# A prologue reordered: inputs by feature chunk, layer norm first, shared expert ahead of the router

## The chip, the cores and the metric

The kernel runs on one core of one Trainium2 chip. The metric is the device time of one execution in microseconds (us), median of several runs. Before the change it is 1330.2 us (three runs, 1329.89 to 1331.93).

## What is computed

A sequence x (8 batches, 512 steps, 256 features, float32) passes through four blocks; each adds its output to x. A second input, cond (8 by 256), steers three of them.

```python
# L0: mixture of experts, one shared (hidden 512), 8 routed (hidden 128), top 2
shared = (silu(x @ sw1.T) * (x @ sw3.T)) @ sw2.T
s = sigmoid(x @ router_w.T + cond @ router_t_w.T)
combine = gates of the two largest s + router_bias, normalised
routed = sum_e combine[e] * (gelu(x @ rw1[e].T) @ rw2[e].T)
x = x + (shared + routed) / 3
# L1: wavelet transform, gate = sigmoid(silu(cond@W1.T+b1)@W2.T+b2), inverse
# L2: low-rank matrices made per batch from cond (layer norm, gelu, then W2 of 8 MB)
# L3: a GRU over the 512 steps
Z = sigmoid(xz + H @ Whz.T); R = sigmoid(xr + H @ Whr.T)
H = Z * H + (1 - Z) * tanh(xh + R * H @ Whh.T);  Y = H @ Whq.T
```

The wavelet step with its inverse comes down to scaling by a gate per feature, so the kernel holds it as the factor `lr2`.

## The kernel before, in words

Features lie on partitions (two chunks k of 128, `KC`), batches and time steps in the free dimension. Time is cut into 16 windows of 32 steps (`WS`, `NW`); a window is 256 columns (8 batches times 32 steps). L0 to L2 of a window are a list of jobs (`window_jobs`); L3 is a loop over 512 steps that needs the window's result.

There are two phases. The **prologue** loads the weights, computes what depends on cond alone (time bias of the router, layer norm and the low-rank matrices of L2, the gate of L1), routes the first four windows (`route`, `EARLY = 4`) and computes window 0. The **recurrence** then runs the GRU step by step and fills the gaps of every step with jobs of later windows.

The order of instructions on each engine is fixed when the program is built. A `Job` has an engine, the jobs that it depends on, the ring buffers that it uses, and an estimated duration (`takes`, and `lag` for transfers). `Jobs.run` (line 179) keeps a clock for each engine and, whenever the clock of an engine has come, emits the first job of its queue that is ready by these estimates. The estimates only choose the order; on the chip each engine works through its own list in order, and semaphores make it wait for what an instruction really needs. So an instruction that waits holds up everything behind it on its engine. A second set of queues, `small`, is not looked at by `run` before the change.

Names and lines that matter here:

- `load_x` (347) loads a stretch of x, one transfer for each chunk k. Block 0 is `x0`, four windows; its first window is loaded first (364), the rest at 367. `sw13_sb` (365) holds sw1 and sw3, loaded as two transfers, one per matrix. Then follow rw1 (371), sw2 (373), wsq_a (375, five square matrices), rw2 (377), and the eight 1 MB pieces of W2 (`pieces`, 380 to 387, tile w, five buffers: a sixth piece waits until an earlier one has been used). I call them w1 to w8. All these go through SP's queue. Small inputs (cond, router, router bias, vecs, bias2 as b) go through ACT's queue, h0 and the bias rows through POOL's.
- `hidden` (525): the two products x·w of a hidden block, into one half of a PSUM pair (tiles hp and low); line 453 is the helper `quads` that issues each product as four matrices of 32 columns. A shared unit (540) is hidden w1, hidden w3, sigmoid on ACT (546), lin and g on DVE (554, 562), then `into_acc` (505) into the accumulator acc. A routed unit (570) is hidden, Erf on ACT (578), gl on DVE (586), g on POOL (594: gl times bc), then `into_acc`.
- `route` (789): logits (799), transpose on DVE (825), sigmoid (829), some twenty small DVE operations for the top 2 (836 to 862), a transpose to cT (825); cT is written to DRAM (comb_d, 877) and read back broadcast to all partitions (bc, 485). For the first four windows (`via_pool`) POOL and ACT issue these.
- layer norm (887 to 940): mean by TensorE (892), diff (903), dsq (907), var (911), square root on ACT (917), `normalize`. `dense_cond` (942) makes hid and the gate, with products at 953 and hid_pre, g_pre, gate_pre at 963.
- the low-rank matrices (1000 to 1061): bias rows (misc<-b, by `quads`), then four uses of the pieces in pairs, (w1, w2) to (w7, w8), at 1023 (misc<-w), low_out (1039), transposes (1048), low_in (1054).
- `jobs.run` at 1074 ends the prologue when window 0's L0, low_in, and the last weights have been placed. The steps after that (window 0's L2, xt, the first projection at 1115) are emitted by the second `run`, at 1231.

Of the kernel before, what the change touches and what calls it, by code (L numbers as in the profile page):

```python
# [9 lines left out]
F32 = mybir.dt.float32  # L10
# [6 lines left out]
P = 128  # L17
B, T, C = 8, 512, 256
KC = C // P
E = 8  # L20
# [116 lines left out]
class Jobs:  # L137
# [41 lines left out]
    def run(self, until):  # L179

        while any(j.done is None for j in until):
            for eng, at in self.clock.items():
                if at <= self.now:
                    job = next((j for j in self.queues[eng] if j.ready(self.now)), None)
                    if job is not None:
                        self.queues[eng].remove(job)
                        job.emit(self.now)
                        self.clock[eng] = self.now + job.takes
# [11 lines left out]
def cond_resid_kernel(  # L200
# [109 lines left out]
    jobs = Jobs()  # L310

# [35 lines left out]
    def load_x(n, mb, some=None):  # L347
# [8 lines left out]
        a, b = (i * WS for i in some)  # L356
        for k in range(KC):
            got = load(t[:, k, :, a:b], xs[:, k, :, t0 + a : t0 + b], mb)
# [5 lines left out]
    load_x(0, 0.25, (0, 1))  # L364
    sw13_sb = const.tile([P, 2, KC, HS], F32, name="sw13_sb")
    got_sw13 = [load(sw13_sb[:, g], rows_of(sw13[g]), 0.5) for g in range(2)]
    load_x(0, 0.4, (1, EARLY))
    got_vec = load(vec, vecs, 0, eng="ACT")
    got_b2 = load(b2[: 4 * R], bias2.rearrange("q (r d) -> (q r) d", d=C), 0, eng="ACT")
    rw1_sb = const.tile([P, KC, E, P], F32, name="rw1_sb")  # L370
    got_rw1 = load(rw1_sb.rearrange("p k e h -> p k (e h)"), rows_of(rw1), 1.0)
    sw2_sb = const.tile([P, HC, C], F32, name="sw2_sb")
    got_sw2 = load(sw2_sb, rows_of(sw2), 0.5)
    wsq_a = const.tile([P, KC, 5, C], F32, name="wsq_a")
# [90 lines left out]
    def window_jobs(w, routed, xt, via_pool=False):  # L465
# [18 lines left out]
        def fetch(i):  # L484
# [12 lines left out]
                lag=LAG,  # L497
# [27 lines left out]
        def hidden(lazy, n, lhs, got):  # L525
            last = None
            for k in range(KC):
                last = mm(
                    lazy,
                    n,  # L530
                    lambda k=k: lhs(k),
                    lambda k=k: x[:, k],
                    k == 0,
                    [last, got, got_x[w]],
                )
            return last
# [3 lines left out]
        for m in range(HC):  # L540
            h, sig, lin, g = bank(), Lazy(r_sig), Lazy(r_lin), Lazy(r_g)
            j1 = hidden(h, 0, lambda k, m=m: sw13_sb[:, 0, k, ts(m, P)], got_sw13[0])
            j3 = hidden(h, 1, lambda k, m=m: sw13_sb[:, 1, k, ts(m, P)], got_sw13[1])
# [26 lines left out]
        for e2 in range(0, E, 2):  # L570
            h = bank()
            for n in range(2):
                e = e2 + n
                j = hidden(h, n, lambda k, e=e: rw1_sb[:, k, e, :], got_rw1)
# [15 lines left out]
                    [h, sig, gl],  # L590
                )
# [153 lines left out]

    prod = set1.tile([P, KC, B, E], F32, name="prod")
# [42 lines left out]
    def route(ws, tiles, psum, via_pool, behind=()):  # L789
# [6 lines left out]
        def products():  # L796
# [12 lines left out]
            products, [*(got_x[w] for w in ws), got_rout_sq, *behind], [logits], 0.45  # L809
# [655 lines left out]
```

## Time and profile before

| | us |
|---|---|
| median of the runs | 1330.2 |
| the profiled execution, its own time | 1334.46 |
| its span, first to last instruction | 1332.2 |
| first product of x (tile hp) | 8.26 |
| transpose of the logits | 16.78 |
| cT done, POOL writes comb_d | 25.32 |
| first routed g on POOL | 36.88 |
| the four uses of pieces of W2 start (PE misc, L1023) | 31.23, 38.12, 42.51, 48.06 |
| window 0's accumulator complete | 53.50 |
| recurrence starts (grh<-wx) | 67.8 |
| mean granted clock of TensorE | 0.984 |

The execution that was profiled took 1334.46 us, 2.3 us more than its span: that much lies around the first and the last instruction. It also lies 4.3 us above the median of the runs.

How to read it: PE is TensorE's matmul row, PEld its weight loads, DVE, ACT and POOL the vector, scalar and GpSimd engines, SP the queue that issues most transfers. A float32 product counts as two instructions per matrix, so a product in `quads` is x8 in the trace. A tile is named without its buffer's number: grh is also the name that small prologue results have (they borrow a bank of it). The chain of waits is followed back from the last instruction; asked for a stretch, it starts from that stretch's end.

### The profile page before, as it was taken

The page shows a single profiled execution, that of the slowest core. Times are in us where ns is not written, and L with a number is a line of the kernel's source. Part 1 is how long each engine was busy: PE and PEld are TensorE (multiplying, and loading weights), DVE is VectorE, ACT ScalarE, POOL GpSimd, SP SyncE. Part 2 cuts the span into 40 slices and gives each one's busy share as a digit, 9 for nine tenths or more (in the row PEclk, how much of TensorE's full clock was granted, in tenths as well). Part 3 has the DMA queues.
Part 4 walks back from the last instruction along what each step waited for, and adds up shares of the span by engine and source line. Part 5 has one row for each costly group of instructions (what it writes and reads, how often), then busy time and mean ns, then how long its engine had stood idle before and what let it go on. Part 6 is the DMA issues. An engine that isn't in the chain of part 4 may idle for free.

```text
span 1332.2 us, 88576 instructions
## 1 busy us (share of the span) xinstructions
PE 1183.3 (89%) x39016; PEld 704.9 (53%) x39016; DVE 914.9 (69%) x6255; ACT 507.3 (38%) x3403; POOL 149.3 (11%) x228
## 2 busy tenths in 40 slices
PE   8999989999898998989898988888888888988885
PEld 4565555555555555555454554545454554555554
DVE  5267777777776767666676767667676766767665
ACT  2143433343343434334343434434343443433332
POOL 3310111101010110101011010101101010110000
PEclk8999999999999999999999999999999999989997
DMA  9910001101010000201000010100001000000111
GB/s 338 330 51 13 4 6 44 44 5 36 5 41 15 20 20 4 52 4 28 12 21 20 4 36 4 28 12 20 20 4 36 4 4 4 5 4 4 36 36 19
DMA packets 41586, 46.44 MB, mean 35 GB/s; under 512 B 27472, under 2 KB 31088, under 8 KB 40048
## 3 DMA queue, kind: packets, MB, share of 16 engines
q1 hardware_dynamic: 38304, 38.31, 9.6%
q8 instruction: 304, 4.98, 1.5%
q0 software_dynamic: 1184, 2.31, 0.6%
q14 instruction: 82, 0.67, 0.2%
q10 hardware_dynamic: 1712, 0.16, 0.1%
HBM read 36.45 MB, written 4.33 MB: 31 GB/s over the span
## 4 chain that ended last, share of the span: by engine, by line
PE 68%; DVE 17%; ACT 8%; issue 5%; DMA 1%; POOL 0%; DVEq 0%; ACTq 0%; POOLq 0%
PE grh L1115 34%; PE hp L453 13%; PE acc L453 8%; DVE rT L1295 6%; DVE d L1295 5%; PE gz L1115 5%; ACT r L1281 5%; PE low L453 4%; ACT c L1281 3%; PE misc L453 3%; DVE s_h L1372 2%; DVE s_rh L1312 2%; DMA brow<-in_bias_rows_dram 0%; DMA bc<-comb_d 0%; PE misc L1023 0%
## 5 line engine op out<-in xcount | busy, mean ns | idle before, releaser
L1281 ACT ACTIVATE r<-grh 128x32 f32<-128x32 f32 x1024 | 146.3, 195 | 439.8 <-PE grh L1115 439.8
L1295 DVE STREAM_TRANSPOSE rT<-r 128x32 f32<-128x32 f32 x1024 | 156.0, 190 | 225.6 <-ACT r L1281 221.6
L1115 PE MATMUL grh<-wh,s_h 128*32 128x64 f32 x8192 | 223.8, 226 | 75.4 <-DVE s_h L1372 74.2
L1115 PEld LDWEIGHTS grh<-wh,s_h 128*32 128x32 f32 x8192 | 145.0, 110 | 274.4 <-DVE s_h L1372 271.2
L1115 PE MATMUL grh<-wh,s_rh 128*32 128x64 f32 x8192 | 223.1, 227 | 52.0 <-DVE s_rh L1312 29.8
L1281 ACT ACTIVATE c<-grh 128x32 f32<-128x32 f32 x1024 | 146.3, 195 | 310.0 <-PE grh L1115 307.6
L1115 PEld LDWEIGHTS grh<-wh,s_rh 128*32 128x32 f32 x8192 | 141.6, 109 | 201.5 <-DVE s_rh L1312 198.9
L1295 DVE STREAM_TRANSPOSE d<-c 128x32 f32<-128x32 f32 x1024 | 156.5, 192 | 119.3 <-ACT c L1281 113.5
L1115 PE MATMUL gz<-wh,s_h 128*32 128x64 f32 x8192 | 212.1, 221 | 1.2 <-issue 1.2
L1115 PEld LDWEIGHTS gz<-wh,s_h 128*32 128x32 f32 x8192 | 155.3, 111 | 1.7 <-issue 1.6
L453 PE MATMUL hp<-x,sw_sb 128*32 128x256 f32 x2016 | 151.8, 389 | 1.7 <-ACT sig L546 1.1
L594 POOL TENSOR_TENSOR g<-gl,bc 128x256 f32<-128x256 f32 x128 | 93.6, 733 | 518.1 <-DVE s_h L1372 355.6
L453 PE MATMUL hp<-x,rw_sb 128*32 128x256 f32 x2016 | 149.6, 380 | 2.3 <-ACT sig L578 1.1
L453 PE MATMUL acc<-g,rw_sb 128*32 128x256 f32 x2048 | 150.2, 379 | 1.6 <-POOL g L594 1.1
L1372 DVE TENSOR_TENSOR_SCAN s_h<-d,d 128x16 f32<-128x16 f32 x1024 | 145.3, 183 | 0.0
L1312 DVE TENSOR_TENSOR s_rh<-rT,s_h 128x8 f32<-128x8 f32 x1024 | 133.1, 167 | 0.0
L1295 DVE STREAM_TRANSPOSE zT<-z 128x64 f32<-128x64 f32 x512 | 121.6, 238 | 1.1 <-ACT z L1281 1.1
L1281 ACT ACTIVATE z<-gz 128x64 f32<-128x64 f32 x512 | 121.0, 236 | 1.9 <-PE gz L1115 1.4
L1115 PE MATMUL grh<-wx,xt 128*32 128x128 f32 x2048 | 106.8, 276 | 3.3 <-ACT r L1281 3.3
L1386 ACT COPY hist<-s_h 128x16 f32<-128x16 f32 x512 | 105.9, 207 | 0.5 <-DVE s_h L1372 0.5
L1324 DVE TENSOR_TENSOR d<-zT,s_h 128x16 f32<-128x16 f32 x512 | 90.8, 177 | 17.6
L1325 DVE TENSOR_SCALAR d<-zT 128x16 f32<-128x16 f32 x512 | 86.8, 170 | 0.0
(151 smaller groups left out, 1193.4 us busy)
## 6 DMA issues: line engine op xcount, KB each, us to landing
bc<-comb_d SPq DMA_DIRECT2D x56, 256.0 KB, 3.2
w<-in_w_dram SPq DMA_DIRECT2D x8, 1024.0 KB, 12.6
out_dram<-x SPq DMA_DIRECT2D x14, 256.0 KB, 3.2
x<-in_xT_dram SPq DMA_DIRECT2D x2, 1536.0 KB
rw_sb<-in_rw_dram SPq DMA_DIRECT2D x2, 1024.0 KB
bc<-comb_d POOLq DMA_DIRECT2D x8, 256.0 KB, 8.4
sw_sb<-in_sw_dram SPq DMA_DIRECT2D x3, 512.0 KB, 6.3
wsq_a<-in_sq_a_dram SPq DMA_DIRECT2D x1, 1280.0 KB
```

The source lines that it names most:

```text
L453: nc.tensor.matmul(out[ts(j, 32)], lhs[:, ts(j, 32)], rhs, start=start, stop=False, skip_group_check=True,)
L594: lambda gl=gl, g=g, e=e: nc.gpsimd.tensor_tensor(g.get(), gl.get(), bcs[e // 2].get()[:, e % 2], ALU.mult),
L1115: nc.tensor.matmul(out[ts(j, 32)], lhs, rhs[:, ..., ts(j, FQ)], start=start, stop=False, skip_group_check=True,)
L1281: nc.scalar.activation(x, y, func)
L1295: ins = nc.vector.transpose(dst.rearrange("p i u b -> p i (u b)"), src.rearrange("p (i r) -> p i r", r=32),)
L1312: prod = tt(s_rh[u][:, k, u, :], rT[:, k, u, :], h[:, k], ALU.mult)
L1324: tt(d1[:, :, u, :, 1], zT[:, :, u, :], h, ALU.mult)
L1325: nc.vector.tensor_scalar(d0[:, :, :, 1], zT[:, :, u, :], -1.0, 1.0, ALU.mult, ALU.add)
L1372: new = nc.vector.tensor_tensor_scan(s_h[v][:, k, v].rearrange("p b w -> p (b w)"), d0[:, k].rearrange("p b w -> p (b w)"), d1[:, k, u].re ...
L1386: nc.scalar.copy(hist[:, :, t, :], s_h[v][:, :, v, :, 1])
```

## The change

It does these things:

1. sw1 and sw3 are loaded by feature chunk: x chunk 0, then chunk 0 of both matrices, x chunk 1, then chunk 1 (`load_sw13`, `between`). The tile's layout changes with it. Products wait only for their own chunk (`got[k]`, `got_x[w][k]`), and the second hidden of a shared or routed pair no longer starts its own accumulation group (`first`).
2. sw2 is loaded ahead of rw1, and rw1 in two halves of four experts each.
3. The layer norm's jobs, up to the square root, are put ahead of the router's. The rest of the normalisation stays where it was.
4. The router's top-2 operations, and gl of window 0, go into the `small` queue, and `run` now looks at `small` after the main queue. So lin, g, hid_pre and the like go ahead of them when ready.
5. Estimates that steer the order are changed: PE's clock starts at 3.5, the lag of the comb_d writes is 1.8 times, that of the bc fetches 2 times what it was, durations of loads are raised.
6. The bias rows of the low-rank matrices (misc<-b) depend on the load of wsq_a as well.

In the order of instructions that comes of it: on PE, misc<-b moves from ahead of the first product to behind the layer norm's dense product; the first products run k = 0 of two units, then k = 1 of both; the router's products come behind the first half of the third unit; routed units of window 0 are done before the accumulations of routed experts, and three of those stand between the third and the fourth use of pieces, five behind the fourth. On ACT, one of three table loads is gone (square root is first), and the comb_d writes move behind three more activations. On POOL, three of the four fetches for window 1 move ahead of the first routed g. On SP, the two sw13 transfers alternate with x. From window 1's first products on, the order is as before.

```diff
@@ Jobs.run
-                    job = next((j for j in self.queues[eng] if j.ready(self.now)), None)
+                    qs = (self.queues[eng], self.small[eng])
+                    ready = ((j, q) for q in qs for j in q if j.ready(self.now))
+                    job, q = next(ready, (None, None))
                     if job is not None:
-                        self.queues[eng].remove(job)
+                        q.remove(job)
@@
     jobs = Jobs()
+    jobs.clock["PE"] = 3.5
@@ load_x
+        got = []
         for k in range(KC):
-            got = load(t[:, k, :, a:b], xs[:, k, :, t0 + a : t0 + b], mb)
+            got.append(load(t[:, k, :, a:b], xs[:, k, :, t0 + a : t0 + b], mb))
+            if between is not None:
+                between(k)
@@
-    load_x(0, 0.25, (0, 1))
-    sw13_sb = const.tile([P, 2, KC, HS], F32, name="sw13_sb")
-    got_sw13 = [load(sw13_sb[:, g], rows_of(sw13[g]), 0.5) for g in range(2)]
-    load_x(0, 0.4, (1, EARLY))
+    sw13_sb = const.tile([P, KC, 2, HS], F32, name="sw13_sb")
+    got_sw13 = []
+
+    def load_sw13(k):
+        rows = sw13[:, ts(k, P), :].rearrange("g p h -> p g h")
+        got_sw13.append(load(sw13_sb[:, k], rows, 0.5))
+
+    load_x(0, 0.6, (0, 1), load_sw13)
+    load_x(0, 0.5, (1, EARLY))
@@
-    rw1_sb = const.tile([P, KC, E, P], F32, name="rw1_sb")
-    got_rw1 = load(rw1_sb.rearrange("p k e h -> p k (e h)"), rows_of(rw1), 1.0)
     sw2_sb = const.tile([P, HC, C], F32, name="sw2_sb")
     got_sw2 = load(sw2_sb, rows_of(sw2), 0.5)
+    rw1_sb = const.tile([P, KC, E, P], F32, name="rw1_sb")
+    half = slice(0, E // 2), slice(E // 2, E)
+    got_rw1 = [
+        load(rw1_sb[:, :, e], rw1.rearrange(...)[:, :, e], 0.5)
+        for e in half
+    ]
@@ fetch of bc
-                lag=LAG,
+                lag=2 * LAG if via_pool else LAG,
@@ hidden
-        def hidden(lazy, n, lhs, got):
-            last = None
+        def hidden(lazy, n, lhs, got, first=None):
+            made = []
             for k in range(KC):
-                last = mm(
+                made.append(mm(
...
-                    k == 0,
-                    [last, got, got_x[w]],
+                    k == 0 and first is None,
+                    [first, *made, got[k], got_x[w][k]],
@@ gl of a routed unit
+                    queue=None if w else jobs.small,
@@ route
-            queue = jobs.queues if via_pool else jobs.small
-            d = jobs.add("DVE", fn, [d, got_rbias], (), takes, queue)
+            d = jobs.add("DVE", fn, [d, got_rbias], (), takes, jobs.small)
...
-        made = []
+        made, lag = [], 1.8 * LAG if via_pool else LAG
@@ layer norm: mean_over_features ... sd0 stand ahead of prod and time_bias, not behind route
@@ biased_rows
-        j = pe(biased_rows, [got_b2], [gp], 0.45)
+        j = pe(biased_rows, [got_b2, got_sq_a], [gp], 0.45)
```

## The prediction

> **What bounds the kernel now.** I read the page first, for which engine carries the end.
>
> ```profile
> PE 1183.3 (89%) x39016; PEld 704.9 (53%) x39016; DVE 914.9 (69%) x6255; ACT 507.3 (38%) x3403; POOL 149.3 (11%) x228
> ...
> PE 68%; DVE 17%; ACT 8%; issue 5%; DMA 1%; POOL 0%; DVEq 0%; ACTq 0%; POOLq 0%
> ```
>
> TensorE is busy for 89% of the span and holds 68% of the chain that ended last. Most of that is the recurrence, from 67.8 us to the end. The order of instructions there is the same before and after: on PE all rows from the window-1 products that follow the last expert's accumulation, on DVE, ACT and POOL likewise. So the change can move the end only by moving the start of the recurrence, and I need the chain up to there. This is the chain of work in order of time (start, duration, what):
>
> ```profile
> 25.32 5.02 DMA comb_d<-cT
> 30.34 0.28 issue
> 30.63 6.12 DMA bc<-comb_d
> ...
> 36.88 0.73 POOL g L594
> ...
> 42.69 1.73 PE misc L1023 x32
> ...
> 48.24 1.73 PE misc L1023 x32
> 49.97 0.86 PE acc L453 x16
> 50.84 0.37 PE grh L1048 x2
> 51.21 2.29 PE acc L453 x40
> 53.50 2.59 PE hp L453 x48
> ...
> 67.79 0.22 PE grh L1115 x8
> ```
>
> The gates cT are written out at 25.32, come back as bc at 36.78, and from 37.66 PE works almost without a break until window 0's accumulator is complete at 53.50. From there to the recurrence at 67.79 are 14.3 us of unchanged steps. Call 53.50 the end of the prologue; that is the number to predict. Next, engines by stretch (PE, PEld, DVE, ACT, POOL busy; granted clock; DMA share; GB/s):
>
> ```profile
> 5.50:9.00 3.50, 2.06 (x24) 1.33 (x23) 0.64 (x4) 0.00 (x0) 2.25 (x5) 0.99 1.06 338
> 9.00:15.80 6.80, 6.29 (x56) 3.05 (x60) 2.36 (x11) 3.16 (x4) 3.20 (x6) 0.50 1.12 347
> ...
> 24.00:31.00 7.00, 6.50 (x92) 4.12 (x91) 4.56 (x21) 1.48 (x5) 0.90 (x2) 1.00 1.01 419
> 31.00:37.00 6.00, 4.97 (x83) 2.61 (x82) 0.54 (x3) 1.33 (x4) 1.96 (x5) 1.00 1.01 418
> 37.00:53.50 16.50, 15.68 (x272) 8.84 (x276) 4.85 (x22) 1.87 (x6) 7.70 (x12) 1.00 0.99 329
> ```
>
> Two things are to be seen. PE has slack at the front: half clock from 9.0 to 15.8, and 1 us idle in 31 to 37. The last column but one is the second limit: the DMA engines are full from 5.5 us on, at 419 GB/s in 24 to 31. The waits of SP's queue name what it carries:
>
> ```profile
> SPq L317 <- PE misc L1023: 12.9, 2, 6.8
> SPq L317 <- DMA wsq_a<-in_sq_a_dram: 9.0, 1, 9.0
> ```
>
> The eight 1 MB pieces w1 to w8 of the low-rank matrix are loaded in five buffers; the sixth and the eighth wait until PE has used earlier ones. By the completion records in the trace w1 to w4 land at 26.36, 28.80, 31.24 and 33.67 (2.44 apart), then, with the bc fetches beside them, w5 36.90, w6 40.93, w7 43.49, w8 47.19. PE's fourth use of pieces (48.24) needs w8, so DMA is only 1 us behind PE there.
>
> **First products (gain).** Before, PE's first product hp stands behind misc<-b, which waits for b (landed 7.69): it starts at 8.26. After, misc<-b is moved behind the dense products and the first products need only half of x and half of sw13. Those land about 6.5 (the first half of sw13 landed at 7.75, behind one more 128 KB of x that took 1.1 us), so PE starts behind the time bias, at 6.7. The second half of sw13 still lands last, 9.48. Products that need it run from 9.5.
>
> **Clock.** The row 9.00:15.80 shows PE busy 6.29 us at clock 0.50: some 3.1 us of work lost. The Trainium skill ("TensorE: Matmul & The Clock Gate", Part 1: The HAM clock gate) says that the clock is halved after an idle window of about 3.4 us. Before, PE was busy 2.06 of 3.5 us ahead of the drop, so a window need not be wholly idle here. After: time bias 0.66, two pairs of products 0.86 each, variance 0.6, together 3.0 of 3.5. By the rule the clock stays full and the router's products end at 13.1 (x's rest lands at 12.45, as now); by the row's half clock they end at 16.2, and the transpose that follows starts then instead of 16.78. I take the full clock. It matters less than it seems, for the next reason.
>
> **Gates (a loss).** DVE works in order. After, three lin/g pairs (0.84 each) stand between the logits and the top-k, and a fourth inside it, against two in all before cT now. Also hid_pre, hid, g_pre and g are now inside the top-k chain (0.32+0.58+0.36+0.17 = 1.4). hid_pre needs the dense product of wsq_a, which lands at 21.46. Step by step: transpose and logit 13.15 to 13.86; three pairs to 16.35; five top-k steps at 0.26 to 17.7; wait for hp's second half, pair to 18.9; seven steps to 20.7; hid_pre waits for 21.46 + 1.06 and ends at 23.0; three steps and hid to 24.4; g_pre behind the next dense product (DVE idle 0.6) at 25.4; the remaining steps and the transpose to 27.6. With the half clock: 28.7. Before: 25.03. So the gates are 2.6 us later in spite of the earlier start. With the trace's own 5.0 + 0.3 and 6.1 us for writing out and fetching, bc lands at 39.1 instead of 36.78.
>
> What queues behind: ACT's three comb_d writes (1.18 us) now stand before sig of the routed products; they end at 28.9, and that sig is not due before 30.4, so nothing now, and 1 us per us if cT came after 29.2. On POOL three fetches for window 1 (0.55 each, 1.65) are moved ahead of the first g; they lie in the wait for bc (4.04 us now), and cost 1.65 without it.
>
> **PE between.** Its work before the first use of w1, w2 ends at 30.3 (they land at 28.80), where it began at 31.23; routed products that stood between the uses come earlier, and the second use ends at 36.4 instead of 40.02. So w8 is issued behind w7 without a gap (now: issued 40.05). The third use waits for w6; three accumulations for g; the fourth use for w8. All of this is done by 43.5, and PE is no longer the limit.
>
> **DMA, the new end.** The bytes are the same. x and sw13 alternate, so large packets run while the many small ones of x are being issued: shares below 1 before 5.5 us leave at most 0.8 us; I take 0.4. Without fetches w8 would land at 33.67 - 0.4 + 4 x 2.44 = 43.0. But now all seven fetches (four before) go out before it. Here a rule speaks against the change: the skill's "DMA: Bandwidth & Descriptors", Queues, rings and completion order, says that each DMA engine takes turns between the queues, a packet (several descriptors) at a time. The trace's turns are single ones: bc lands 1.2 to 2.1 us apart, that is four 4 KB pieces of 0.13 and as many 8 KB of 0.30 (1.7). From 37.0, when fetches arrive, (43.0 - 37.0)/0.305 = 20 pieces of w are still to come per engine, each paying one turn of 0.13: 2.6 us, w8 at 45.6. By the rule's larger packets the fetches, 28 pieces of 0.13, would all be ahead: 46.6. I take the row: 45.6.
>
> From the fourth use on, the rows above give 1.73 + 0.86 + 0.37, then four accumulations: 64 instructions where 40 took 2.29, so 3.66; 6.6 in all. 45.6 + 0.3 (landing to first product) + 6.6 = 52.5, against 53.50: **1.0 us earlier**. The profiled execution took 1334.46 (span 1332.2), so it would be 1333.5; on the median of the runs, 1330.2, it is 1329.2.
>
> Unknown costs: the start of DMA (0 to 0.8, so 0.4 either way), the turns (0 to 28 pieces: -2.6 to +1.0), the length of a turn (next paragraph). The three added lin/g and hid moves cost at most the 2.6 us of gates already counted.
>
> **Rivals.** (a) Faster: fetches get few turns before w8. It speaks for this that in the trace most bc packets passed in 34 to 37, when w5 had run out on most engines. But the three accumulations in front of the fourth use need two fetches, 8 turns: w8 is at 44.0 at best, the end 50.9, time 1327.6. If they were starved altogether, g would come after 44 and the gain would be gone again; so this is a limit. An even larger gain needs gates earlier than my DVE count.
> (b) Slower: turns are long. Between 45 and 47 us, when fetches met small packets, the 35 gate pieces begun took 0.42 us each, and DMA moved 170 GB/s from 46 to 47 where it had moved 402 from 35 to 36. If the three added fetches, 12 turns per engine, pay 0.29 more each: 3.5 us, w8 at 49.1, end 56.1, time 1332.8. It decides as soon as w8 lands after 46.6.
> (c) The change doesn't start PE earlier, since the first halves land with the second ones at 9.5: then gates come 1 us later still, fetches take fewer turns, and w8 is at 45; end 51.9, time 1328.6, or up to 1330 if PE is late.
>
> **How the numbers follow.** My forecast with (c), a shift between -2 and +1 us: 0.57. (a): 0.23. (b): 0.20. A measurement of this kernel can tell about 0.2% (2.7 us) from no change. Cases of (a) reach past that only if PE and gates too are better than counted, and of (b) if all turns are long (up to +5), but both have room for steps I mis-sized: faster 0.26, same 0.56, slower 0.18. Range: from (a) with 2 us beyond its limit, 1325.7, to (b), 1333.0.
>
> **What would show it.** First hp at 6.7 us, clock 1.00 from 9 to 16; cT written out at 27.7 and hid_pre waiting for PE; bc at 39; SP's wait for the eighth piece gone; the fourth use (misc x32) starting at about 46 on a DMA wait; accumulation complete at 52.5, recurrence at 66.8. I am wrong if w8 lands far from 45.6, if the fourth use waits for POOL instead, or if the stretch behind the start of the recurrence changes its length by more than a microsecond.

## The result, and the profile after

The changed kernel took 1335.3 us (median of seven runs, 1333.83 to 1338.29) beside 1331.93 us of the kernel before in the same session (seven runs, 1329.89 to 1334.27): a ratio of 1.0025, 95% interval 1.0013 to 1.0036, that is 1.7 to 4.8 us slower. Twelve more runs of it in a later session (e20, below) gave 1.0012, interval 0.9998 to 1.0027. So the change costs something like 2 us where 1.0 us of gain was forecast. Its profiled execution took 1335.25 us, its span is 1332.6.

The page first, engines and chain as before:

```profile
PE 1183.1 (89%) x39016; PEld 701.4 (53%) x39016; DVE 914.7 (69%) x6255; ACT 504.8 (38%) x3402; POOL 149.4 (11%) x228
...
PE 68%; DVE 17%; ACT 8%; issue 4%; DMA 2%; SPq 0%; DVEq 0%; ACTq 0%
```

Averages tell nothing of it: the shares are those of before, and a loss of 2 us in 1330 cannot show in them. The chain of work in order of time (start, duration, what) does:

```profile
36.24 1.75 PE misc L1050 x32
37.99 11.15 DMA w<-in_w_dram
49.15 0.04 issue
49.19 1.71 PE misc L1050 x26
...
51.11 0.86 PE acc L473 x14
51.98 0.37 PE grh L1075 x2
52.34 3.59 PE acc L473 x64
55.94 2.59 PE hp L473 x48
...
70.22 0.22 PE grh L1142 x8
```

Before, the same stretch was the gates' round trip and then PE without a break. Now it is one DMA: w8, issued at 37.99, lands at 49.15; the fourth use of pieces starts 0.04 us later; what PE has left takes 6.79 us; the accumulator is complete at 55.94 and the recurrence starts at 70.22, 14.28 us later, as before. This is the bound that the prediction named, with nearly the tail that it named (6.6), and complete 3.4 us later than it said (52.5). The stretches (columns as before: PE, PEld, DVE, ACT, POOL busy; granted clock; DMA share; GB/s):

```profile
0.50:5.50 5.00, 4.31 (x36) 2.03 (x36) 2.70 (x22) 1.28 (x1) 4.69 (x13) 1.00 0.58 117
5.50:9.00 3.50, 2.34 (x25) 1.70 (x24) 0.63 (x4) 0.00 (x0) 1.76 (x4) 0.92 1.05 264
9.00:15.80 6.80, 6.80 (x98) 3.40 (x97) 2.64 (x13) 2.64 (x5) 3.70 (x7) 0.79 1.13 313
...
31.00:37.00 6.00, 6.00 (x120) 3.60 (x114) 0.51 (x2) 1.15 (x3) 2.75 (x5) 1.00 1.01 392
37.00:53.50 16.50, 12.91 (x184) 6.53 (x180) 4.25 (x16) 1.26 (x4) 7.28 (x12) 0.90 1.03 348
```

PE is ahead now: 6.80 busy of 6.80 from 9 to 15.8 (clock 0.79; before 6.29 at 0.50), 6.00 of 6.00 in 31 to 37; and then it waits, 12.91 of 16.50 where it had 15.68. The last column tells where the loss begins. Between 5.5 and 15.8 DMA moves 264 and 313 GB/s where it moved 338 and 347, though its share is above 1 in these rows, before and after: full, but of smaller packets. Times the lengths, that is 3.05 MB instead of 3.54. The first row sets some of it off. Before, it read:

```profile
0.50:5.50 5.00, 4.31 (x36) 2.12 (x36) 2.72 (x22) 1.28 (x1) 4.69 (x13) 1.00 0.57 91
```

So up to 5.5 us the change gains 0.13 MB, 0.3 us at 419 GB/s, as forecast (0.4); then it loses 0.49 MB, 1.2 us. The net is 0.9 us at 15.8, and w4 lands 1.4 us later, at 35.04; where the other half microsecond arises, these rows do not show. Two more views, DVE's and POOL's timeline (start, length, instruction, and in brackets the idle time before it and its releaser):

```profile
23.96 0.36 DVE L990 TENSOR_SCALAR hid_pre<-grh,vec 128x8 f32<-128x8 f32 x2 [1.12 <-PE grh L980]
...
28.23 0.45 DVE L885 STREAM_TRANSPOSE cT<-gates 128x256 f32<-128x256 f32 x1
```

```profile
42.89 1.42 POOL L622 TENSOR_TENSOR g<-gl,bc 128x256 f32<-128x256 f32 x2 [4.80 <-DMA bc<-comb_d]
```

hid_pre stands in the top-2 chain and waits there for the product of wsq_a, as forecast; cT ends at 28.68. But the first g starts at 42.89 (36.88 before), not at 39.2: the fetch of bc, issued at 34.25, took 8.5 us where it had taken 6.1. So a second limit stands close behind w8. SP's wait for PE has become shorter, from 12.9 us in two waits to 9.0, and that has bought nothing.

### The profile page after: what moved, and what is told of

Same layout as the page of the kernel before. It is cut to its first block, busy times and chain, and to the rows that moved or that the text cites. A ratio compares the mean times of both kernels' runs of the same rounds, so it can differ in the third digit from the quotient of the medians.

```text
span 1332.6 us, 88577 instructions
## 1 busy us (share of the span) xinstructions
PE 1183.1 (89%) x39016; PEld 701.4 (53%) x39016; DVE 914.7 (69%) x6255; ACT 504.8 (38%) x3402; POOL 149.4 (11%) x228
## 4 chain that ended last, share of the span: by engine, by line
PE 68%; DVE 17%; ACT 8%; issue 4%; DMA 2%; SPq 0%; DVEq 0%; ACTq 0%
PE grh L1142 34%; PE hp L473 13%; PE acc L473 8%; DVE rT L1322 6%; DVE d L1322 5%; PE gz L1142 5%; ACT r L1308 4%; PE low L473 4%; ACT c L1308 3%; PE misc L473 3%; DVE s_h L1399 2%; DVE s_rh L1339 2%; DMA wsq_a<-in_sq_a_dram 1%; DMA w<-in_w_dram 1%; DMA sw_sb<-in_sw_dram 0%
## 5 line engine op out<-in xcount | busy, mean ns | idle before, releaser
L473 PE MATMUL hp<-x,sw_sb 128*32 128x256 f32 x2016 | 148.5, 383 | 2.1 <-ACT sig L571 1.1
## 6 DMA issues: line engine op xcount, KB each, us to landing
w<-in_w_dram SPq DMA_DIRECT2D x8, 1024.0 KB, 13.3
```

The lines of the kernel that those rows point to most:

```text
L473: nc.tensor.matmul(out[ts(j, 32)], lhs[:, ts(j, 32)], rhs, start=start, stop=False, skip_group_check=True,)
```

## The experiments

The theory (T): the end of the prologue is the landing of w8 plus PE's work behind the fourth use; w8 is late through a slower load stream and through the fetches' turns. The rivals: late gates hold PE and POOL (R); the three fetches for window 1 that now go out early make w8 late (F); the loss lies in the recurrence (C). The table gives, from the completion records and the chain of each trace, the landing of w4, of the first bc and of w8, the start of the fourth use (its bulk, where its first products could start early), the completion of the accumulator and the start of the recurrence; then the ratio to the kernel before, with its interval, where it was timed in rounds.

| kernel | w4 | bc | w8 | fourth use | complete | recurrence | ratio |
|---|---|---|---|---|---|---|---|
| before, shown above | 33.67 | 36.74 | 47.19 | 48.24 | 53.50 | 67.79 | |
| before: e14 | 34.03 | 37.15 | 47.44 | 50.12 | 55.38 | 69.66 | |
| before: e23 | 33.52 | 36.82 | 46.18 | 48.33 | 53.58 | 67.87 | |
| before: e24 | 33.67 | 36.88 | 48.03 | 48.38 | 53.63 | 67.92 | |
| changed, shown above | 35.04 | 42.75 | 49.15 | 49.19 | 55.94 | 70.22 | 1.0025 (1.0013 to 1.0036) |
| changed: e13 | 34.78 | 42.81 | 48.11 | 48.15 | 54.90 | 69.19 | |
| changed: e20 | 34.91 | 43.96 | 49.10 | 49.14 | 55.88 | 70.17 | 1.0012 (0.9998 to 1.0027) |
| e1 fetches late | 34.43 | 43.65 | 47.99 | 49.72 | 55.41 | 70.13 | |
| e2 rw1 in 4 KB | 34.47 | 43.33 | 48.25 | 48.29 | 55.04 | 69.33 | |
| e4 gates early | 35.43 | 36.96 | 50.37 | 50.42 | 57.16 | 71.45 | 1.0025 (1.0013 to 1.0036) |
| e5 fourth use late | 34.89 | 44.93 | 49.37 | 52.92 | 56.88 | 71.17 | 1.0010 (0.9999 to 1.0021) |
| e6 before, bias moved | 34.01 | 37.06 | 48.69 | 48.56 | 54.23 | 68.52 | 0.9993 (0.9974 to 1.0011) |
| e7 e5, e2, e1 together | 35.17 | 43.81 | 48.55 | 50.67 | 54.63 | 70.16 | 1.0026 (1.0012 to 1.0041) |
| e9 gates behind | 35.19 | 42.87 | 48.51 | 48.55 | 62.15 | 76.45 | |
| e10 e4 and e5 | 35.26 | 36.12 | 49.35 | 52.19 | 56.15 | 70.44 | 1.0028 (1.0011 to 1.0045) |
| e11 e10, e2, e1 | 34.59 | 36.18 | 46.81 | 51.80 | 55.76 | 70.96 | 1.0023 (1.0013 to 1.0034) |
| e15 dense behind | 34.76 | 38.03 | 51.62 | 52.59 | 58.27 | 72.56 | 1.0036 (1.0022 to 1.0049) |
| e18 all moved | 35.15 | 38.21 | 48.93 | 48.83 | 53.13 | 67.85 | 1.0002 (0.9988 to 1.0016) |
| e19 e18, early fetches | 34.57 | 38.05 | 53.53 | 53.57 | 59.39 | 73.68 | 1.0017 (1.0006 to 1.0029) |
| e22 loads as before | 34.08 | 44.06 | 48.27 | 49.20 | 55.75 | 70.04 | 1.0004 (0.9988 to 1.0020) |

A run's time varies by some 8 to 10 us from one execution to the next (the kernel before, 35 runs in one session: 1327.3 to 1337.9), so single times decide nothing here. The ratios over many runs do. The stamps of the prologue do where they differ by more than the traces of one kernel among themselves; most variants have one trace only. From complete to the recurrence are 14.3 us in sixteen of the twenty traces; the other four are those with late fetches (e1, e7, e11, e18), with 14.72 to 15.53.

**How firm the stamps are (e14, e23, e24: the kernel before again; e13, e20: the changed one again).** No edit.

> The kernel before, once more, for how much its own time stamps vary between executions: w4 landed at 33.67, bc first at 36.74, w8 at 47.19, accumulator complete at 53.50. Expected within 0.5 us of each. If w4 lands at 34.4 to 35, the slower load stream of the changed kernel lies within what an execution varies by.

> The changed kernel, once more, for how much its own time stamps vary between executions. In its first trace: cT written out at 28.96, w4 landed at 35.04, bc first at 42.75, w8 at 49.15, accumulator complete at 55.94, recurrence at 70.2. The kernel before gave 53.50 and 55.38 in two executions, the later one with half a clock on TensorE from 38 to 42 behind a wait for the gates. Theory T2 (w8 and the gates both hold the end): w8 at 48.4 to 49.4, complete at 55.2 to 57. If the kernel before and the changed one differ only by what an execution varies by: complete at 53.5 to 55.

> The changed kernel in five more rounds against the kernel before, and a third trace. Its first seven runs gave a ratio of 1.0025 (1.0013 to 1.0036), 3.4 us. In the two traces of each, the recurrence starts at 67.79 and 69.66 before, at 70.22 and 69.21 after: 1.0 us later in the mean. Theory T2 (the loss is the later end of the prologue): ratio 1.0008 to 1.0020, 1 to 2.7 us. If the first ratio stands (1.0025 or more), a part of the loss lies elsewhere than in the start of the recurrence.

> A third trace of the kernel before, to set beside three of the changed kernel (accumulator complete at 55.94, 54.90, 55.88; w8 at 49.15, 48.11, 49.10, the fourth use 0.04 us behind it each time). The first two of the kernel before were complete at 53.50 and 55.38, and differ by half a clock behind the wait for the gates. Theory T2: w4 at 33.6 to 34.1, w8 at 47 to 48, complete at 53.4 to 55.5, and the mean of the traces 0.8 to 2 us ahead of the changed kernel's, as the timed runs say (1.2 to 2.5 thousandths).

> A fourth trace of the kernel before; the same as for the third. If both were complete at 55 or later, the later end of the prologue could not be the loss that the timed runs show.

Four traces of before give 53.50, 55.38, 53.58 and 53.63, mean 54.02; three of the changed kernel 55.94, 54.90 and 55.88, mean 55.57: 1.55 us later. The ranges overlap, and e13, at 54.90, lies where I had put two kernels that differ by chance only (53.5 to 55); it is the means and the timed runs together that speak for a later end. e14 missed the half microsecond that I had allowed, and shows why; its chain:

```profile
38.07 1.08 PE acc L453 x8
39.15 2.76 PE misc L1023 x32
...
55.38 2.59 PE hp L453 x48
```

The first use behind the gates takes 2.76 us where it took 1.73. PE had waited 2.18 us for g, and half a clock followed. And e13, a microsecond ahead of the other two traces of the changed kernel:

```profile
48.15 1.71 PE misc L1050 x26
...
51.31 3.59 PE acc L473 x64
54.90 2.59 PE hp L473 x48
```

All of that microsecond is w8, which landed at 48.11. From the landing to the end are 6.79, 6.79 and 6.78 us in the three traces: this part of T is as firm as anything here. C finds no support: from the first r on ACT to the last instruction are 1262.7, 1261.4, 1259.6 and 1259.9 us before, 1260.7, 1259.6 and 1262.5 after, in both the mean 1260.9, though single traces differ by 3 us. What is left of the size: 1.55 us by the traces, 1.6 and 3.4 by the timed runs. I take the loss to be near 2 us, and all of it ahead of the recurrence.

**Is it the fetches (e1)?** The window-1 fetches come behind the last g of window 0 on POOL:

```diff
-                [routed[w % EARLY]],
+                [routed[w % EARLY], got_low_in[1] if via_pool and w else None],
```

> The changed kernel, but the fetches of window 1's gates (bc) are issued by POOL only behind window 0's last routed g, so they no longer take turns with the pieces of W2. One accumulation also moves ahead of the fourth use of pieces. In the changed kernel w8 landed at 49.15 us, the fourth use started at 49.19, the accumulator was complete at 55.94. Theory T (the end of the prologue is the landing of w8 plus 6.8 us of PE's work; w8 is late through a slower load stream and through the turns of window 0's own fetches): w8 at 48.5 to 49.2, complete at 54.5 to 55.1, most of that from the moved accumulation (0.86). Rival F (the three added fetches are what makes w8 late): w8 at 47.5 or earlier, complete at 53.6 or earlier. Rival R (the late gates hold PE, not w8): complete at 55.9 as now.

w4 to w8 is 13.56 us here; 14.11, 13.33 and 14.19 with the three fetches. So they cost about 0.3 us in the mean, less than the 0.9 by which those three traces differ: F is not the cause of a loss of 1.6 us in w8. (w8 itself landed at 47.99, between the two ranges, because w4 was early.) But the end came at 55.41, not at 54.5 to 55.1: PE waited 2.85 us for the first g and went on at half clock (64 instructions in 5.16 us). Here R had a part of it.

**Is it the gates (e4)?** The top-2 operations of the early windows return to the main queue:

```diff
-            d = jobs.add("DVE", fn, [d, got_rbias], (), takes, jobs.small)
+            d = jobs.add("DVE", fn, [d, got_rbias], (), takes, jobs.queues if via_pool else jobs.small)
```

> The changed kernel with the router's top-2 operations of the first windows back in the main queue, so that the gates cT are complete at about 24 to 25 us instead of 28.7 and bc lands some 4 us earlier; loads unchanged, what PE has left behind the fourth use nearly unchanged (6.8 us). Theory T: the fetches then take their turns earlier, but as many of them; w8 within 1 us of 49.15, accumulator complete within 1 us of 55.9, time as the changed kernel's within 1.5 us. Rival R (late gates hold PE and POOL): complete at 53 or earlier, 3 us or more faster than the changed kernel.

```profile
39.77 1.75 PE misc L1050 x32
41.52 8.85 DMA w<-in_w_dram
...
57.16 2.59 PE hp L473 x48
```

bc lands 5.8 us earlier and the end comes 1.2 us later, with w8, at the very ratio of the changed kernel. (w8 and the end are 0.2 to 0.3 us outside T's ranges, the time inside.) The simple form of R falls: the fetches only meet the pieces sooner (w5 lands at 38.96 instead of 37.48).

**What if PE uses the wait for w8 (e5)?** Its accumulations go ahead of the fourth use:

```diff
+            sums.append(order[0])
...
+        if w == 0:
+            last_use.deps.append(sums[HC + 5])
```

> The changed kernel with the fourth use of pieces planned behind the sixth routed accumulation, so that the accumulations which need no piece of W2 are done while PE would wait for w8; only the fourth use, what follows from it and the last accumulations stay behind. Loads and gates unchanged. Theory T: w8 lands as in the changed kernel (48.7 to 49.5), the accumulator is complete at 52.6 to 53.6 instead of 55.94, the recurrence starts at 67.0 to 67.8 instead of 70.2, and the time is 2.4 to 3.3 us below the changed kernel's, level with the kernel before (ratio 0.999 to 1.001). Rival R (gates hold PE): PE waits for g instead, complete at 55 or later. Rival C (the loss lies in the recurrence or its clock, not in its start): the start moves as in T, but the time stays at the changed kernel's, 1.0025 of the kernel before.

```profile
37.13 7.80 DMA bc<-comb_d
...
45.07 0.73 POOL g L624
...
45.85 7.07 PE acc L473 x96
52.92 1.73 PE misc L1054 x32
...
56.88 2.59 PE hp L473 x48
```

The chain is no longer w8's. PE stands 3.01 us for the first g, then needs 7.07 us for 96 instructions (5.2 at full clock), and the fourth use starts 3.5 us after w8 has landed. The gates were 1.5 us later than in the changed kernel's first trace, at that. So T as I had put it falls too, and the end is where R had it (55 or later): w8 is one of two limits, and the other is close behind. The time came down as T had it (1.0010), with an interval that reaches from no loss to the changed kernel's.

**Both at once (e10), and with the load edits too (e11).** The edits of e4 and e5; e11 adds those of e1 and e2.

> The changed kernel with both edits of two earlier runs: top-2 operations in the main queue (gates at 24.5 us instead of 28.7) and the fourth use behind the sixth routed accumulation. Alone, the first left the end where w8 put it (w8 50.4, complete 57.2), the second moved the end to the wait for the gates (first accumulation at 45.9, half clock behind it, complete 56.9). Theory T2 (w8 and the gates are two limits of nearly the same time; each edit alone meets the other one): w8 at 49.5 to 50.5, one accumulation, transposes and one accumulation behind the fourth use, complete at 53.5 to 54.5, 2.5 to 3.5 us below the run with early gates alone, time level with the kernel before (0.999 to 1.001). If PE's own work or its clock were the limit: complete at 56 or later, ratio about 1.002.

> The run with early gates and late fourth use, and beside it rw1 in runs of 4 KB and the fetches for window 1 behind the last g of window 0: everything that the theory of two limits asks for. Theory T2: w8 at 47.8 to 49.0 (about 0.8 us for the three fetches, about 0.5 for the load stream), complete at 51.8 to 53.0, recurrence from 66.1 to 67.3, time 0.5 to 1.7 us below the kernel before (ratio 0.9987 to 0.9996). If the later fetches for window 1 are missed by the first steps of the recurrence: the start as said, and the time level with the kernel before or above.

Both missed; e10's 56.15 and 1.0028 are near what I had put for PE itself as the limit. In e11 w8 lands at 46.81, 2 us ahead of the changed kernel, and nobody waits for it:

```profile
24.00:31.00 7.00, 6.30 (x48) 3.57 (x48) 3.22 (x15) 0.81 (x3) 1.68 (x4) 0.53 1.01 420
```

```profile
49.01 1.07 PE hp L473 x16
50.08 1.73 PE acc L473 x32
51.80 1.73 PE misc L1054 x32
...
55.76 3.00 PE hp L473 x51
```

With the top 2 first, DVE gives lin, g and hid_pre late; PE has several waits of 0.4 to 0.6 us near 21 to 24, drops to half clock (0.53 from 24 to 31, 48 instructions where the changed kernel does 108), and its own work is the third limit, ending at 55.76.

**The late gates, with all else moved (e7).** The edits of e5, e2 and e1.

> The changed kernel, gates as late as in it, with the fourth use of pieces behind the sixth routed accumulation, rw1 in runs of 4 KB, and the fetches for window 1 behind the last g. The late gates leave first g at about 43.6 and last g at 48.5 to 49.5. Theory of limits: w8 at 47.0 to 48.0 without the three fetches, but the gates hold the sixth accumulation until 48.5 to 50, so complete at 52.3 to 54.5 (the spread is whether TensorE falls to half clock while it waits for the first g), ratio 0.9995 to 1.001, 1 to 3 us below the changed kernel. If w8 alone were the limit: complete at 51.5, ratio 0.998 to 0.999.

w8 lands at 48.55, half a microsecond later than put, and nobody waits for it: g, behind a bc that landed at 47.80, starts at 47.96, two accumulations follow, and the fourth use at 50.67. The gates hold the end, at 54.63. That was said, but the ratio was not: 1.0026 does not go with an end 0.9 us ahead of the changed kernel's mean. The chain behind the end shows where that went:

```profile
54.63 3.00 PE hp L473 x51
57.63 0.43 issue
58.05 0.41 PE hp L473 x3
...
70.16 0.22 PE grh L1147 x8
```

Eight more hp instructions stand there than in the changed kernel (56, not 48: 0.43 us) and PE pauses for 0.43 us, so the recurrence starts at 70.16, as late as in the changed kernel (mean 69.86). The late fetches change that order: e1, e11 and e18 have the 56 as well. Where the last 0.4 us of the 1.24 lies is not located. Here the start of the recurrence, not the end of the accumulator, goes with the ratio.

**A middle way on DVE (e15), and all three limits moved (e18, e19).** Only the operations of the dense products go behind the top 2; lin and g stay ahead:

```diff
-        return pre, dve(add_bias, [j, got_vec], [ps], 0.4)
+        return pre, jobs.add("DVE", add_bias, [j, got_vec], [ps], 0.4, jobs.small)
...
```

e18 and e19 add the third use behind the third and the fourth behind the sixth routed accumulation, and rw1 in 4 KB; e18 the late fetches.

> The changed kernel with one part of its fourth step taken back: DVE's operations of the dense products of cond (hid_pre, hid, g_pre, g, gate_pre) go behind the router's top-2 operations, so that the gates no longer wait for wsq_a on DVE; lin and g of the shared units stay ahead. The two waits (1.12 and 0.82 us) and those operations (about 1.5 us) leave the chain to cT: comb_d issued at 25.2 to 26 instead of 28.96, bc first at 38 to 40 instead of 42.75. PE keeps its early products (unlike the run with all top-2 operations first, where PE became the limit at half clock). Theory T2: the fetches then delay the pieces earlier, w8 at 48.7 to 50.4; accumulations of the first four experts done before the fourth use, which starts with w8; one accumulation, transposes and three accumulations behind it, 5.6 us: complete at 54.4 to 56; time within 1.5 us of the changed kernel's. If the gates alone held the end: complete at 53 or earlier, ratio 1.000 or below.

> Every one of the three limits moved: the dense operations behind the top 2 on DVE (gates at 25.5), the third use of pieces behind the third and the fourth use behind the sixth routed accumulation (PE accumulates while w6 and w8 are on their way), rw1 in runs of 4 KB, and the fetches for window 1 behind window 0's last g. Theory of three limits (w8, gates, PE's order): w8 at 46.6 to 47.8 (46.8 with the same loads and early gates), fourth use within 0.5 us of it, 3.9 us of work behind it: complete at 50.6 to 52.0, recurrence at 65 to 66.5, against 67.8 and 69.7 in the two traces of the kernel before; time 1.5 to 3.5 us below the kernel before (ratio 0.9974 to 0.9989), if the first steps of the recurrence do not wait for the later fetches; if they do (a run with early gates had a recurrence about 3 us longer than the others), level with the kernel before. If the theory is wrong: complete at 54 or later.

> As the run with all three limits moved, but with the fetches for window 1 where the changed kernel has them, ahead of the first g. Theory of three limits: w8 at 48.0 to 49.4 (1.2 to 2 us later than with the later fetches), complete at 52.0 to 53.4, recurrence at 66.3 to 67.8; time level with the kernel before to 2 us below (ratio 0.9985 to 1.0003). The difference to the run with later fetches is what the three fetches cost w8, if the recurrence's length is the same in both.

None of the three met its numbers but for bc, at 38.0. In e15 comb_d was issued at 27.92, 1 us earlier than in the changed kernel and not 3; and bc came early mainly because w had nothing to send then. hid is later here, so the first use of pieces moves from 31.92 to 33.26, its buffer comes free later, and w6 is issued at 35.01 instead of 33.68: by the packets of the trace, the pieces' queue moves next to nothing from 36 to 38. PE's timeline in e15:

```profile
33.08 1.91 PE L1050 MATMUL misc<-w,hid 128*32 128x256 f32 x32
...
44.99 3.20 PE L1050 MATMUL misc<-w,hid 128*32 128x256 f32 x26 [3.42 <-DMA w<-in_w_dram]
```

w6 lands at 44.94 (42.00 in the changed kernel), PE waits 3.42 us and loses its clock. e19 has the same and waits for w8 besides:

```profile
40.33 13.20 DMA w<-in_w_dram
...
53.57 3.20 PE misc L1056 x26
...
59.39 2.59 PE hp L473 x48
```

e18 differs from it only by the late fetches:

```profile
46.24 2.59 PE acc L473 x48
48.83 1.85 PE misc L1056 x30
...
52.13 1.00 PE acc L473 x16
53.13 3.02 PE hp L473 x56
```

w4 to w8: 18.96 against 13.79. Between these two traces the three fetches cost 5.2 us, where e1 had found 0.3. F, wrong for the change, is right next to it: all seven fetches and an eighth are in front of w8 there, 32 packets of 4 KB per DMA engine against 16, by my count of the packets between the two landings (23 to 27 in the changed kernel). But this is one trace of each: the starts of the recurrence are 5.8 us apart, the medians of the timed runs only 2.7 (1335.66 and 1332.98), so 5.2 is not the usual price. e18 is the best that I found, with PE and w8 meeting within 0.1 us: complete at 53.13, 1.1 us beyond the range, recurrence at 67.85, and a ratio of 1.0002. It takes the loss back, and no more.

**The load stream (e2, e22).** e2 lays out rw1 so that each half has runs of 4 KB; e22 loads x, sw13 and rw1 as before the change:

```diff
-    load_x(0, 0.6, (0, 1), load_sw13)
+    load_x(0, 0.6, (0, 1))
+    got_m = [load(sw13_sb[:, :, g], rows_of(sw13[g]), 0.5) for g in range(2)]
...
+    got_rw1 = [load(rw1_sb.rearrange("p k e h -> p k (e h)"), rows_of(rw1), 1.0)] * 2
     sw2_sb = const.tile([P, HC, C], F32, name="sw2_sb")
```

> The changed kernel with rw1 laid out so that each of its two transfers has runs of 4 KB per partition instead of 2 KB (as the packets of rw1 were before the change); the order of instructions is the same. In the changed kernel rw1's halves moved at about 307 GB/s and w4 landed at 35.04 us (33.67 before the change). Theory T (load stream): rw1's second half, wsq_a, rw2, w1 to w4 all land 0.6 to 1.0 us earlier, w8 at 48.1 to 48.6, accumulator complete at 54.9 to 55.4. If the size of the packets is not what slowed this stretch: w4 at 34.9 to 35.1, and complete at 55.9. Rival R (gates bound the end): loads earlier, complete at 55.9 all the same.

> The changed kernel with the loads as before the change: x and sw13 per matrix, rw1 whole and ahead of sw2. The planned order stays that of the change but for a few products and lin/g pairs. w4 landed at 33.67 and 34.03 before, at 35.04 and 34.78 after. If the new load order is what slows the stream: w4 at 33.6 to 34.2, w8 0.7 to 1.2 us earlier than the changed kernel's, at 47 to 48; complete at 53.8 to 55; time 0.5 to 1.5 us below the changed kernel's. If the stream is slow for another reason: w4 at 34.7 or later and no gain.

e2 met its numbers but for 0.03 us, w4 at 34.47 and complete at 55.04; but e1 had w4 at 34.43 without that edit. A hit that a kernel without the edit makes as well shows nothing: rw1's second half landed at 18.78, against 19.05 in e1, and what the size of its packets is worth stays open. e22 is clear on the stream:

```profile
5.50:9.00 3.50, 2.86 (x18) 2.32 (x21) 0.80 (x5) 0.20 (x1) 2.20 (x5) 1.00 1.03 342
9.00:15.80 6.80, 6.29 (x76) 2.92 (x72) 2.15 (x10) 2.06 (x4) 3.25 (x7) 1.00 1.12 343
```

342 and 343 GB/s again, w4 at 34.08, next to the spread of before (33.52 to 34.03), 0.8 us ahead of the changed kernel's mean. The other traces agree: the six with the loads as before have w4 at 34.08 or earlier, the fourteen with the new order at 34.43 or later. The time is 1.0004, with an interval that holds both no loss and the 1.0012 of the changed kernel. w8, at 48.27, and the end missed their ranges:

```profile
44.98 4.22 PE acc L459 x48
49.20 1.73 PE misc L1036 x32
...
55.75 2.59 PE hp L459 x48
```

The gates had it again: 3.19 us of waiting for g, half clock, and the fourth use 0.9 us behind w8. So the load order makes w4 late; that putting it back would take back the end is not shown.

**What PE's earlier start is worth alone (e6).** In the kernel before, misc<-b depends on wsq_a, nothing else:

```diff
-        j = pe(biased_rows, [got_b2], [gp], 0.45)
+        j = pe(biased_rows, [got_b2, got_sq_a], [gp], 0.45)
```

> The kernel before with the sixth step of the change alone: misc<-b also depends on wsq_a, so PE's first products no longer stand behind the load of b. First hp at 7.5 to 7.8 instead of 8.26 (it waits for sw13 then), all else as before. The limit of the kernel before at its end is PE's order behind the gates, with w8 1 us behind it: complete at 52.5 to 55.4 (53.50 and 55.38 in two traces of the kernel before), ratio 0.999 to 1.001. If the start of PE were worth what it moves: 0.5 us or more earlier everywhere, ratio 0.9995 or below.

Its first hp starts no earlier than before (8.7, and not 7.5 to 7.8: sw13 landed at 8.56 in this execution), and the ratio, 0.9993, is not to be told from 1. The products cannot use a start that the loads do not allow.

**Piece and fetch apart (e9).** The fetches were to wait for w8:

```diff
-                [routed[w % EARLY]],
+                [routed[w % EARLY], pieces[LOW[1][-1], 1][1] if via_pool else None],
```

> The changed kernel with every early fetch of the gates (bc, seven transfers) issued by POOL only when w8 has landed. It measures what the fetches cost the pieces of W2: w4 to w8 was 14.1 us in the changed kernel (13.5 before the change, with four fetches in it) and would be 4 x 2.44 = 9.8 us alone. Theory T (turns between the queues): w8 lands 9.8 to 10.4 us behind w4, near 44.5 to 45.2; the fourth use starts there; the gates then arrive after 50, so the accumulator is complete late, at 58 to 61, and the time is 3 to 6 us above the changed kernel's. If w8 is late for another reason (issue by SP, the buffers of w): w8 still 12 us or more behind w4.

It did not do what it was made for. A dependency in the plan gives the order of emission only; on the chip an instruction waits for what it reads, and a fetch reads nothing of w8: POOL issued the first at 35.01. w8 landed 13.3 us behind w4, as ever. What the fetches cost together was thus not measured by itself. But all eight accumulations had gone behind the fourth use:

```profile
48.55 3.65 PE misc L1050 x28
...
53.39 8.76 PE acc L473 x128
62.15 2.59 PE hp L473 x48
```

The end moved to 62.15, and the one run took 1342.39 us, 7 us above the changed kernel's median, with a recurrence that starts 6.6 us later than the changed kernel's mean: what stands behind w8 does count.

## Why the prediction was wrong

**First products.** Forecast 6.7, measured 7.32: the first half of sw13 landed at 7.18, not 6.5, the second at 10.45, not 9.48. Right in kind; the loads were late already here.

**Clock.** Forecast full. It was half from 8.5 to 11.9, between the two cases. PE had been busy for 2.34 us of the stretch from 5.5 to 9, and for 2.25 of the 3.41 us ahead of the drop, so the rule of the Trainium skill ("TensorE: Matmul & The Clock Gate", Part 1: The HAM clock gate), taken as asking for an idle window, does not describe it; the row did, as before. As forecast, it mattered little in this trace; in e20 the half clock lasted 6.8 us, and cT came at 29.44.

**Gates.** Forecast cT at 27.6, or 28.7 with the half clock: 28.68. That agreement is luck: hid_pre waited, as named, for the product of wsq_a, and wsq_a landed at 22.82 where 21.46 had been carried over. The late stream came last there, 1.1 us behind DVE's own work, and not the clock. And bc was put at 39.1 with the 6.1 us of before's fetch, and came at 42.75 (8.5 us). What the forecast missed is an order: before, POOL issued the fetch at 30.63 and SP w6 at 33.20; after, w6 went at 33.68 and the fetch at 34.25. In the eleven traces in which the fetch was issued ahead of w6 it took 4.3 to 7.0 us, in the nine in which it came behind, 7.7 to 9.0.

**PE between.** Forecast: PE no longer the limit. Right: 12.91 busy of 16.50.

**DMA, the new end.** This step failed: "33.67 - 0.4", and "each paying one turn of 0.13: 2.6 us". Both terms of the landing of w8:

| | forecast | changed, mean of three | before, mean of four |
|---|---|---|---|
| w4 landed | 33.27 | 34.91 | 33.72 |
| four pieces alone | 9.76 | 9.76 | 9.76 |
| added by fetches and gaps | 2.6 | 4.1 | 3.7 |
| w8 landed | 45.6 | 48.8 | 47.2 |

The stream was forecast 0.4 us faster and was 1.2 us slower: 1.6 of the 3.2 us. I had thought that large packets would fill the time of the small ones. Up to 5.5 us they did, for 0.3 us. But in the trace, by its packets, chunk 0 of sw13 runs ahead of x's second chunk, whose 128-byte packets are then late, and between 9 and 12 us the 384-byte packets of x have nothing large beside them, where rw1's 4 KB packets ran before. e22 shows that the order of the loads makes w4 late; which of its parts does more is not settled.

The turns were forecast at 2.6 and were 4.1: the other 1.5. The row was in the trace of before: w4 to w8 took 13.52 us there with little more than four fetches in it (18 packets of 4 KB per DMA engine), so 3.76 over the bare pieces. I replaced this sum by 20 turns at 0.13 us, though seven fetches should not take less than four. The price was too low: in both traces the median such packet took 0.16 us, and the mean between w4 and w8 is 0.19. Nor does a count give the answer: 16 packets cost 3.8 us in e1, 23 to 27 cost 4.1 here. With 3.76 and the forecast stream, w8 is at 46.8, past the point (46.6) that rival (b) gave for itself. Against before only 0.4 us of the delay of w8 is of this kind. The larger packets of the rule in the Trainium skill ("DMA: Bandwidth & Descriptors", Queues, rings and completion order) would have put w8 at 46.6. That is nearer, but not for its reason: the fetches landed 0.9 to 2.0 us apart, where four packets of 0.16 in a row take 0.6, and the last three landed behind w8, at 49.32 to 51.37.

**Tail and rest.** 6.6 forecast, 6.79 measured; 14.3 and 14.28. Right.

**Rivals.** (b) gave w8 at 49.1, the end at 56.1 and 1332.8; the first trace had 49.15 and 55.94. It had the place and the number, the number by luck: its long turns of the three added fetches are worth about 0.3 us there (e1). (a) and (c) did not come.

So the change did what it says: PE starts earlier, and from 37 on it has 3.6 us of idle time where it had 0.8. The gain went to nobody, because PE's order, the gates and w8 had been within 2 us of each other, and the change made both others later: the gates by 6 us, through DVE's new order (3.6 us) and a longer fetch (2.4), w8 by 1.6, of which 1.2 is the load stream, through its new order (e22). That the loss is all of w8's making is not shown: moved alone, each of these limits met the next.

## What to carry to other kernels

Where several limits lie within a few microseconds, moving work off one of them buys at most the distance to the next, and must not be paid with the others: list for each engine and queue when it would be ready for the joint that ends the stage, before and after. Where a stretch of the trace holds the very quantity that is forecast (four loads with their interference, end to end), start from it and add to it; a count of parts at their best price came out below what had already been measured. A wait on TensorE can cost more than its length: in e14 2.18 us of waiting were followed by 3.4 us at half clock.

## What the runs showed of the hardware

- In eight traces waits of TensorE of 2.08 to 3.84 us were followed by half clock: for 3.4 us in six of them, 1.7 us of work lost (the row from 37 us on reads 0.90 where one such stretch lies in 16.5), for 6.8 us in e15, and for 10.2 us in e9, which has three waits in a row (1.65, 2.15 and 2.87). Single waits of 1.5 and 1.6 us in e7, e13 and e20 were not. Several waits of 0.4 to 0.9 us in a row were followed by 6.8 us at half clock in e4, e10 and e11.
- The row of the granted clock can miss a stretch at the start of the trace: in e5, e18 and e24 its record begins at 16.0 to 16.6 us, and it reads 1.00 from 5.5 to 15.8, with no instruction of hp below 604 ns there and 634 in the median, the length that it has at half clock (378 at full). In e1, e2, e11, e14 and e22 the record begins at 13.5 to 13.8, so the 1.00 in e22's rows above is not to be trusted either. The length of one instruction is the better witness.
- In the changed kernel's trace the first 4 KB packets of bc took 0.46, 0.39 and 0.29 us in the mean at 37, 38 and 39 us, and 0.16 from 41 on. Before, where the fetch was issued ahead of w6, they took 0.16 from the first, at 33 us. What makes some slow stays open.
- A fetch of bc issued ahead of w6 took 4.3 to 7.0 us (eleven traces), one issued behind it 7.7 to 9.0 (nine).
